# Attention's start, its last weights and its last sums: a reordering on one Trainium2 core

## The chip, the cores and the metric

One core of a Trainium2 chip runs the whole program as a single launch. The metric is the device time of that launch in microseconds (us); lower is better. TensorE is called PE here, VectorE DVE, ScalarE ACT, GpSimd POOL, and SyncE SP; SP issues most of the DMAs.

## The reference

The input `x` holds 64 sequences of 32 positions with 512 features, 2048 rows in all, in fp32. Four layers follow, each `x = x + ffn(cond(x))`. The first is a product chosen per sequence and a feed-forward block, the second a low-rank adapted gated block with a mixture. The change lies in the code of the third and fourth. Cut to what matters:

```python
# layer 2: attention over a paged cache of 512 keys and 32 own keys
q, k = rope(rmsnorm(x @ Wq.T)), rope(rmsnorm(x @ Wk.T))    # 32 and 8 heads of 128
v = x @ Wv.T
s = q @ concat(k_cache[block_table], k).T * SCALE          # masked by length
o = softmax(s) @ concat(v_cache[block_table], v)
y = o @ Wo.T
x = x + (y @ W_base.T + b_base + low_rank_experts(y))      # layer 2's feed-forward
z = einsum('bct,bcd->bdt', x, weights[subjects])           # layer 3
x = x + (z @ W.T + bias + sum_e coeff_e * z @ A_e.T @ B_e.T)
```

## The kernel before, in words

Rows are held in 16 tiles of 128 (`NT`), four sequences to a tile. Layers 0 and 1 come first and end at 1073 us of the profile. Attention follows, and then the tail (`Tail`), which is layer 2's feed-forward and layer 3.

**Attention** works in two halves of the heads, so that there are 32 steps (half, tile), taken in 16 pairs. Projections and output products of a pair are made by a scheme of seven block products (`ORDER`) in place of eight, with sums of blocks ahead of them and of results behind them. Weights and their sums come from HBM in pieces of 512 KB (`wp_piece`, `wo_piece`).

*One turn* is one group of four query heads of one sequence: scores (`scores`, two matmuls, L993), softmax (minimum and mask on DVE L998, exponential on ACT L1000, reciprocal L1002 and scaling L1005 on DVE), four transpositions of the probabilities (`turned`, L707) and the product with the values (`values`, L712). A step has 16 turns, and each turn has two *slots*, into which pieces of other work are put by hand: products of the next pair's projections, output products of the last pair, loads. So a pair has 64 slots. The order on TensorE is written out: `on_pe` chains each matmul to the one before it. On the other engines the Tile framework places instructions by readiness and program order. DMAs that go through `load_by` (L100) are chained on SP, each to be issued behind the last; those that go through `load` or a plain `nc.sync.dma_start` are not.

Keys of a sequence come as 16 pages of 64 KB (`load_keys`), into one of two buffers `kt`; they are asked for when the buffer's last scores have been issued, in slot 2 of each eight and the two behind it (`keys_of`, `later`). Values come by four gathers on POOL (`load_values`, L738).

**The start of attention** (L1093 to L1156) is written out separately, since nothing can hide it: the first pair's 21 products (`products`, seven each of keys and values, first and second query group), the rotations that follow some of them (`rotated`: DVE L782, L770, L785, L771; POOL L786, L130, L787), the transpositions of the rotated keys and queries (`p.turned(g, i, n)`, L707, copied out by ACT), the first pages (`load_keys`), the first values (`values_of`), the copies of the own values (`own_values_of`, eight on DVE, L745), and the first two scores (`start`). Each of `products` makes, per product, two matmuls of 128x512 (four records), an addition or a copy out of PSUM (DVE L872, or ACT L864; PSUM has two such buffers), and asks for the next weight piece.

**The end of attention**: during the last pair there is no next pair to project, and the tail's weights are loaded in five groups (`Tail.weights`, L1303): A3 and B3; W3T; cat2 and B2; base2T; the two biases. In slots 43 to 61 A3 and B3 are multiplied and added to W3T (`scaled`, `fold`). After the last turn `first_sums(nc.vector)` (L925) makes two block sums of the last outputs, ten output products follow, and then the tail runs.

Of the kernel before, what the change touches and what calls it, by code (L numbers as in the profile page):

```python
# [33 lines left out]
P = 128  # L34
# [630 lines left out]
def attention(c, known, x_in, y_part, y_out, sums, tail):  # L665
# [18 lines left out]
    with ExitStack() as outer:  # L684
# [230 lines left out]
        class Outputs:  # L915
# [9 lines left out]
            def first_sums(self, engine):  # L925
                self.o = [oTs.pop(2 * self.n + i) for i in range(2)]
                (_, _), (o21, o22) = self.blocks = [(o[:, :KH, :], o[:, KH:, :]) for o in self.o]
                self.s = qp.tile([P, KH, P], F32, name="o_sum", bufs=1)
                engine.tensor_tensor(self.s, o21, o22, ALU.add)  # L929
                engine.tensor_tensor(o21, self.blocks[0][0], o21, ALU.subtract)  # L930

            def next_sum(self, m, u):
# [182 lines left out]
        def products(n):  # L1115

            for i in range(count[0], count[0] + n):
                p.product(i // 7, p.ORDER[i % 7])
                if i >= 7 and p.ORDER[i % 7] in (7, 4):
                    held.extend(soon)  # L1120
                    del soon[:]
                the_rest()
                if i < 3 * 7 - 8 or i >= 3 * 7 - 4:
                    next_wp()
            count[0] += n
# [1 line left out]
        count = [0]  # L1127
        products(4)
        load_keys(0, 0, range(2))
        products(3)  # L1130
        load_keys(0, 0, range(2, 4))
        with tc.issue_after(p.last_pool):
            values_of(0)
        for i in (0, HKP):
            own_values_of(i)
        products(3)
        p.turned(0, 0, 0)
        products(4)
        new_keys(0, 1)
        load_keys(0, 1, range(2))  # L1140
        p.turned(0, 1, 0)
        p.turned(1, 0, 0)
        own_keys(0, 0, p.kT[0])
        products(1)
        start(0)
        products(1)
        p.turned(1, 0, 1)
        load_keys(0, 1, range(2, 4))
        products(1)
        start(1)  # L1150
        with tc.issue_after(p.last_pool):
            values_of(HKP)
        projections[1].load()
        products(4)
        p.turned(2, 0, 0)

        def slot(fs):
# [9 lines left out]
        for s, (h, T) in enumerate(steps):  # L1167
# [11 lines left out]
            if s % 2 == 0:  # L1179
                if s == 0:  # L1180
                    p = projections[0]
                    at(1, partial(p.turned, 2, 0, 1), partial(own_keys, 0, 1, p.kT[0]))
                    for i, f in zip((2, 4, 6, 8), held):
                        at(i, f)
                    for i, what in ((9, (1, 1, 1)), (11, (1, 1, 0)), (19, (2, 1, 1)), (25, (2, 1, 0))):
                        at(i, partial(p.turned, *what))
                if not last_pair:
                    p = projections[n + 1]
                    if n == 0:
                        ats = ((12, 14, 16, 17, 18, 20, 22), (24, 26, 28, 32, 33, 34, 38),  # L1190
                               (40, 42, 44, 48, 49, 52, 56))
                        then = ((0, 0, 0, 21), (0, 1, 0, 29))
                        for i, f in zip((3, 5, 6, 7, 10), (partial(p.x, 0), partial(p.x, 1), p.x_sums,
                                                           partial(p.tables, "k"), partial(p.tables, "q"))):
                            at(i, f)
                    else:
                        ats = ((2, 4, 10, 12, 14, 18, 20), (22, 28, 30, 34, 36, 38, 40),
                               (42, 44, 46, 50, 52, 54, 58))
                        then = ((0, 0, 0, 13), (0, 1, 0, 27))
                        at(3, partial(p.tables, "q"))  # L1200
                    for *what, i in (*then, (1, 0, 0, 37), (1, 0, 1, 43), (1, 1, 1, 51), (1, 1, 0, 53),
                                     (2, 0, 0, 57), (2, 0, 1, 65), (2, 1, 1, 67), (2, 1, 0, 73)):
                        at(i, partial(p.turned, *what))
                    for g in range(GB):
                        for m, i in zip(p.ORDER, ats[g]):
                            at(i, partial(p.product, g, m), partial(later.append, next_wp))
                            if g and m != 1 and m != 5 and m != 6:
                                at(i, partial(put_off, s * 2 * per + i + 1 + WAIT[m], waiting))
                    if n + 2 < len(projections):
                        then = projections[n + 2]  # L1210
                        for i, f in zip((30, 40, 59, 61, 62), (then.load, partial(then.tables, "k"),
                                                               partial(then.x, 0), partial(then.x, 1),
                                                               then.x_sums)):
                            at(i, f)
                else:
                    for i, f in zip((4, 8, 12, 16, 20), tail.weights(xp, wk, op, wp_tile)):
                        at(i, f)
                    at(43, tail.scaled)
                    for m, i in enumerate((45, 48, 49, 61)):
                        at(i, partial(tail.fold, ps, m))  # L1220
                    at(52, outputs[n].first_blocks)
                    for i, where in enumerate((52, 54, 57, 59)):
                        at(where, partial(outputs[n].product, i), partial(later.append, next_wo))
                if n:
                    out = outputs[n - 1]
                    at(0, partial(out.first_sums, nc.gpsimd))
                    if out.h:
                        at(14, out.befores)
                    ats = (0, 1, 5, 9, 13, 16, 17, 21, 25, 29, 32, 33, 37, 41) if last_pair else \
                        (0, 1, 6, 8, 16, 17, 24, 26, 32, 33, 48, 49, 56, 60)  # L1230
                    for i, where in enumerate(ats):
                        at(where, partial(out.product, i), partial(later.append, next_wo))
                        if i in (5, 7):
                            for u in range(2):
                                at(where, partial(out.next_sum, 6 if i == 5 else 3, u))
                    at(47 if last_pair else 63, out.store)
                else:
                    for i in (40, 46, 52, 58):
                        at(i, next_wo)
# [35 lines left out]
class Tail:  # L1275
# [28 lines left out]
    def weights(self, x_pool, work_pool, pool, pair):  # L1304

        c, nc, a = self.c, self.c.nc, self.c.a

        def updates():
            self.A3 = x_pool.tile([P, 2, KC, P], F32, name="A3", tag="xT").rearrange("p n k f -> p n (k f)")
            self.B3 = x_pool.tile([P, 4, KC // 2, P], F32, name="B3", tag="x_sums") \  # L1310
                .rearrange("p (n a) k f -> p n (a k f)", n=2)
            for t, n in ((self.A3, "A3"), (self.B3, "B3")):
                nc.sync.dma_start(t, a[n].rearrange("(k p) n -> p k n", p=P))

        def square(name):
            src = a[name].rearrange("(k p) n -> p k n", p=P)
            ts = [pair(name) for _ in range(2)]
            for i, t in enumerate(ts):
                nc.sync.dma_start(t, src[:, 2 * i:2 * i + 2, :])
            return [t[:, k, :] for t in ts for k in range(2)]  # L1320

        def last():
            self.w3 = square("W3T")

        def low_rank():
            src = a["cat2"].rearrange("(k p) n -> p k n", p=P)
            n = src.shape[2]
            self.cat = []
            for k in range(0, KC, 2):
                t = work_pool.tile([P, REP, HD], F32, name="cat2", tag="swapped", bufs=2)  # L1330
                t = t.rearrange("p h d -> p (h d)")[:, :2 * n].rearrange("p (k n) -> p k n", n=n)
                nc.sync.dma_start(t, src[:, k:k + 2, :])
                self.cat += [t[:, 0, :], t[:, 1, :]]
            self.wB = work_pool.tile([P, REP, HD], F32, name="B2", tag="squares").rearrange("p h d -> p (h d)")
            nc.sync.dma_start(self.wB, a["B2"])

        def base():
            self.base = square("base2T")

        def biases():  # L1340
            self.bias = {n: c.load(x_pool, n, [P, D], a[n].to_broadcast([P, D]), tag="xt", bufs=2)
                         for n in ("bias2", "bias3")}

        return updates, last, low_rank, base, biases

# [259 lines left out]
```

## Time and profile before

| what | us |
|---|---|
| median of three runs | 3589.3 (3585.83 to 3597.19) |
| profiled execution, its own time | 3603.64 |
| its span | 3601.9 |
| PE busy in it | 3526.7 |
| DVE, POOL, ACT busy in it | 2154.5, 1598.8, 1301.2 |
| idle time of PE that the timeline shows before its instructions | 71.5 |
| of that, from 1073 to 1150 us | about 12 |
| of that, from 3280 to 3440 us | about 16 |
| mean granted TensorE clock | 0.993 |

How to read it: in a timeline a line gives the start, the duration, the engine, the line of the kernel, the operation, the tile written and the tiles read, and the number of merged instructions; a bracket gives the idle time of that engine before it and what ended it. A table by stage gives, per stretch, its length, the busy time and count of PE, of its weight loads, of DVE, ACT and POOL, then the clock that TensorE was granted (1.00 is full), the share of the DMA engines that was busy, and GB/s.

### The profile page before, as it was taken

The page shows a single profiled execution, that of the slowest core. Times are in us where ns is not written, and L with a number is a line of the kernel's source. Part 1 is how long each engine was busy: PE and PEld are TensorE (multiplying, and loading weights), DVE is VectorE, ACT ScalarE, POOL GpSimd, SP SyncE. Part 2 cuts the span into 40 slices and gives each one's busy share as a digit, 9 for nine tenths or more (in the row PEclk, how much of TensorE's full clock was granted, in tenths as well). Part 3 has the DMA queues.
Part 4 walks back from the last instruction along what each step waited for, and adds up shares of the span by engine and source line. Part 5 has one row for each costly group of instructions (what it writes and reads, how often), then busy time and mean ns, then how long its engine had stood idle before and what let it go on. Part 6 is the DMA issues. An engine that isn't in the chain of part 4 may idle for free.

```text
span 3601.9 us, 61460 instructions
## 1 busy us (share of the span) xinstructions
PE 3526.7 (98%) x19328; PEld 2634.1 (73%) x19328; DVE 2154.5 (60%) x5268; ACT 1301.2 (36%) x3110; POOL 1598.8 (44%) x1607
## 2 busy tenths in 40 slices
PE   8999999999998999999999999999999999999999
PEld 3444788877875777787787777877877778777755
DVE  5443222222227777778778677787787777877433
ACT  1111111111113545444454454444544544444311
POOL 0112332222207546456455464564564655644232
PEclk9999999999999999999999999999999999999999
DMA  5003543333226777888877878788878788877731
GB/s 210 27 26 136 174 135 125 103 103 105 101 72 213 249 243 249 256 248 257 255 248 253 258 247 255 249 257 258 255 254 263 245 264 253 256 253 223 217 94 63
DMA packets 610340, 715.99 MB, mean 199 GB/s; under 512 B 61826, under 2 KB 469378, under 8 KB 610018
## 3 DMA queue, kind: packets, MB, share of 16 engines
q1 hardware_dynamic: 557538, 539.01, 48.2%
q0 software_dynamic: 50176, 168.86, 13.4%
q10 hardware_dynamic: 2304, 4.20, 0.3%
q8 instruction: 157, 2.57, 0.3%
q14 instruction: 165, 1.35, 0.1%
HBM read 669.88 MB, written 41.94 MB: 198 GB/s over the span
## 4 chain that ended last, share of the span: by engine, by line
PE 84%; DVE 8%; DMA 3%; issue 2%; POOL 1%; ACT 1%; SPq 1%; DVEq 0%; another core or an unknown queue 0%; ACTq 0%; POOLq 0%
PE po L712 12%; PE gate_up L366 11%; PE py L712 11%; PE sc L993 10%; PE pq L712 7%; PE prT_ps L707 5%; PE pkv L712 5%; PE pz L366 5%; PE po L1371 3%; PE ph L126 3%; PE pd L251 3%; PE po L366 2%; PE qkT_ps L707 1%; PE py L206 1%; DVE pr L1005 1%
## 5 line engine op out<-in xcount | busy, mean ns | idle before, releaser
L738 POOL DMA_INDIRECT vt<-in_v_rows,v_rows x512 | 510.9, 998 | 313.3 <-PE po L712 189.8
L1000 ACT ACTIVATE pr<-pr,low 128x544 f32<-128x544 f32 x512 | 383.3, 749 | 688.1 <-DVE low L998 556.3
L993 PE MATMUL sc<-kt,qT 128*128 128x288 f32 (+1 forms) x2048 | 557.2, 395 | 15.5 <-DVE low L998 12.6
L993 PEld LDWEIGHTS sc<-kt,qT 128*128 128x128 f32 x2048 | 386.2, 191 | 232.2 <-issue 129.3
L712 PE MATMUL po<-prT,vt 128*128 128x128 f32 x4096 | 546.9, 277 | 4.8 <-ACT prT L1011 3.1
L712 PEld LDWEIGHTS po<-prT,vt 128*128 128x128 f32 x4096 | 522.3, 192 | 39.6 <-ACT prT L1011 20.7
L998 DVE CUSTOM_DVE_ANT_0 pr<-sc,mask 128x544 f32<-128x544 f32 x512 | 368.4, 719 | 142.9 <-PE sc L993 119.2
L786 POOL TENSOR_TENSOR projected<-projected,swapped 128x512 f32<-128x512 f32 x160 | 208.3, 1302 | 313.5 <-DVE projected L785 284.5
L1005 DVE TENSOR_SCALAR pr<-pr,low 128x512 f32<-128x512 f32 x512 | 318.4, 622 | 12.6
L1011 ACT COPY prT<-prT_ps 128x512 f32<-128x512 f32 x512 | 294.0, 574 | 75.3 <-PE sc L993 30.8
L707 PE MATMUL prT_ps<-ident,pr 128*128 128x128 f32 x2048 | 312.5, 275 | 1.8 <-DVE pr L1005 1.7
L707 PEld LDWEIGHTS prT_ps<-ident,pr 128*128 128x128 f32 x2048 | 238.5, 142 | 10.4 <-issue 2.1
L712 PE MATMUL py<-wo,oT 128*128 128x256 f32 x1024 | 241.8, 379 | 0.0
L712 PE MATMUL pq<-wp,x_sums 128*128 128x512 f32 x512 | 240.2, 593 | 0.0
L1002 DVE RECIPROCAL low<-low 128x1 f32<-128x1 f32 x512 | 82.1, 160 | 229.7 <-ACT pr L1000 195.3
L712 PEld LDWEIGHTS py<-wo,oT 128*128 128x128 f32 x1024 | 186.5, 190 | 21.1
L1003 ACT ACTIVATE own_pr<-pr,low 128x32 f32<-128x32 f32 x512 | 164.8, 322 | 93.6 <-DVE low L1002 68.5
L452 DVE TENSOR_TENSOR sg<-sg,gate_up 128x256 f32<-128x256 f32 (+1 forms) x88 | 37.0, 421 | 269.3 <-ACT sg L451 265.9
L130 POOL TENSOR_TENSOR rs<-rs,minus_half 128x4 f32<-128x4 f32 x160 | 180.6, 1129 | 23.3 <-DVE low L1002 15.7
L712 PE MATMUL py<-wo,o_sum 128*128 128x256 f32 x768 | 182.9, 382 | 2.3 <-DVE o_sum L929 2.3
L712 PE MATMUL pq<-wp,xT 128*128 128x512 f32 x384 | 182.2, 597 | 0.2 <-issue 0.2
L745 DVE COPY own_vt<-v 32x128 f32<-32x128 f32 x512 | 164.1, 320 | 22.8 <-issue 4.0
(242 smaller groups left out, 5856.2 us busy)
## 6 DMA issues: line engine op xcount, KB each, us to landing
kt<-in_kT SPq DMA_DIRECT2D x2048, 64.0 KB
wp<-in_sums SPq DMA_DIRECT2D x192, 512.0 KB
wo<-out_sums SPq DMA_DIRECT2D x128, 512.0 KB
wp<-in_WqT SPq DMA_DIRECT2D x96, 512.0 KB
wo<-in_WoT SPq DMA_DIRECT2D x96, 512.0 KB
wp<-in_WkT SPq DMA_DIRECT2D x32, 512.0 KB
xt<-x SPq DMA_DIRECT2D x48, 256.0 KB
in_sums<-sums POOLq DMA_DIRECT2D x24, 512.0 KB, 5.1
```

Source lines behind the costliest of these rows:

```text
L130: self.nc.gpsimd.tensor_tensor(t, t, self.minus_half[:, :n], ALU.pow)
L366: c.on_pe(nc.tensor.matmul(out, lhsT, rhs, start=start, stop=stop))
L707: c.on_pe(nc.tensor.transpose(pt[:, m, :], piece, c.ident))
L712: c.on_pe(nc.tensor.matmul(out, lhsT, rhs, start=first and i == 0, stop=last and i == len(pairs) - 1))
L738: nc.gpsimd.indirect_dma_start(out=vts[b % 2][:, n, :], out_offset=None, in_=a["v_rows"], in_offset=bass.IndirectOffsetOnAxis(ap=rows[h][: ...
L786: nc.gpsimd.tensor_tensor(src, src, tmp, ALU.add)
L993: c.on_pe(nc.tensor.matmul(sc[:, lo + n * PSIZE:lo + m * PSIZE].rearrange("p (n k) -> p n k", k=PSIZE), q, kt[:, n:m, g, :], start=True, s ...
L998: nc.vector.tensor_tensor_reduce(pr[:, :NK], sc[:, lo:lo + NK], masks[h, b], -SCALE, 3.0e38, ALU.add, ALU.min, low[:, 0:1])
L1000: nc.scalar.activation(pr[:, :NK], pr[:, :NK], AF.Exp, bias=low[:, 0:1], scale=-1.0, accum_out=low[:, 1:2])
L1003: nc.scalar.activation(own_prs[b % 2][:, g * S:(g + 1) * S], pr[:, L:NK], AF.Copy, scale=low[:, 2:3])
L1005: nc.vector.tensor_scalar(pr[:, :L], pr[:, :L], low[:, 2:3], None, ALU.mult)
L1011: last_prT.append(nc.scalar.copy(prT, pt).ins)
```

## The change

There are three parts.

1. At the start of attention all 14 products of keys, values and the first query group are made before the first transposition; before it was ten, the transposition of the first keys, and four more. The second half of the first pages is asked for after product 9 instead of 7. The own-value copies are placed after product 9, and the first gathers of values after product 14. Behind that the order becomes: one product between each transposition, the first scores after product 17 (15 before), the second after product 20 (17 before). The second sequence's pages, second half, are asked for after product 17 instead of 16.
2. The tail's weight loads all go through `load_by`, and their slots are 6, 14, 38, 46 and 54 instead of 4, 8, 12, 16 and 20. The contents, tiles and tags stay.
3. The first of the last two block sums, where DVE makes it, is made in two halves of 512 elements instead of one of 1024. The sums on POOL, of the other 15 pairs, stay whole.

```diff
-                engine.tensor_tensor(self.s, o21, o22, ALU.add)
+                for q in (slice(0, KH),) if engine is nc.gpsimd else (slice(0, QH), slice(QH, KH)):
+                    engine.tensor_tensor(self.s[:, q], o21[:, q], o22[:, q], ALU.add)
                 engine.tensor_tensor(o21, self.blocks[0][0], o21, ALU.subtract)
...
         products(4)
         load_keys(0, 0, range(2))
-        products(3)
+        products(5)
         load_keys(0, 0, range(2, 4))
+        for i in (0, HKP):
+            own_values_of(i)
+        products(5)
         with tc.issue_after(p.last_pool):
             values_of(0)
-        for i in (0, HKP):
-            own_values_of(i)
-        products(3)
+        new_keys(0, 1)
         p.turned(0, 0, 0)
-        products(4)
-        new_keys(0, 1)
         load_keys(0, 1, range(2))
-        p.turned(0, 1, 0)
-        p.turned(1, 0, 0)
         own_keys(0, 0, p.kT[0])
         products(1)
+        p.turned(0, 1, 0)
+        products(1)
+        p.turned(1, 0, 0)
+        products(1)
+        load_keys(0, 1, range(2, 4))
         start(0)
         products(1)
         p.turned(1, 0, 1)
-        load_keys(0, 1, range(2, 4))
-        products(1)
+        products(2)
         start(1)
         with tc.issue_after(p.last_pool):
             values_of(HKP)
         projections[1].load()
-        products(4)
+        products(1)
         p.turned(2, 0, 0)
...
-                    for i, f in zip((4, 8, 12, 16, 20), tail.weights(xp, wk, op, wp_tile)):
+                    for i, f in zip((6, 14, 38, 46, 54), tail.weights(xp, wk, op, wp_tile)):
                         at(i, f)
...
             for t, n in ((self.A3, "A3"), (self.B3, "B3")):
-                nc.sync.dma_start(t, a[n].rearrange("(k p) n -> p k n", p=P))
+                c.load_by(t, a[n].rearrange("(k p) n -> p k n", p=P))
...
             for i, t in enumerate(ts):
-                nc.sync.dma_start(t, src[:, 2 * i:2 * i + 2, :])
+                c.load_by(t, src[:, 2 * i:2 * i + 2, :])
...
-                nc.sync.dma_start(t, src[:, k:k + 2, :])
+                c.load_by(t, src[:, k:k + 2, :])
...
-            nc.sync.dma_start(self.wB, a["B2"])
+            c.load_by(self.wB, a["B2"])
...
-            self.bias = {n: c.load(x_pool, n, [P, D], a[n].to_broadcast([P, D]), tag="xt", bufs=2)
-                         for n in ("bias2", "bias3")}
+            self.bias = {n: x_pool.tile([P, D], F32, name=n, tag="xt", bufs=2) for n in ("bias2", "bias3")}
+            for n, t in self.bias.items():
+                c.load_by(t, a[n].to_broadcast([P, D]))
```

## The prediction

> **What bounds the kernel now.** I read the page first: TensorE is busy 98% of the span and carries 84% of the chain that ended last.
>
> ```profile
> PE 3526.7 (98%) x19328; PEld 2634.1 (73%) x19328; DVE 2154.5 (60%) x5268; ACT 1301.2 (36%) x3110; POOL 1598.8 (44%) x1607
> PE 84%; DVE 8%; DMA 3%; issue 2%; POOL 1%; ACT 1%; SPq 1%; DVEq 0%; another core or an unknown queue 0%; ACTq 0%; POOLq 0%
> ```
>
> No matmul is added or removed, so the change can win only PE's idle time, 71.5 us by the brackets of its timeline, and the slow matmuls that follow it. I then read PE's timeline where the change works. The start:
>
> ```profile
> 1094.90 0.65 PE L707 MATMUL qkT_ps<-ident,projected 128*128 128x128 f32 x4 [2.08 <-POOL projected L787]
> 1102.97 0.66 PE L707 MATMUL qkT_ps<-ident,projected 128*128 128x128 f32 x4 [0.55 <-POOL projected L787]
> 1107.04 0.66 PE L707 MATMUL qkT_ps<-ident,projected 128*128 128x128 f32 x4 [3.41 <-POOL projected L787]
> 1116.66 5.31 PE L712 MATMUL pq<-wp,x_sums 128*128 128x512 f32 x12
> 1127.91 0.66 PE L707 MATMUL qkT_ps<-ident,projected 128*128 128x128 f32 x4 [1.92 <-POOL projected L787]
> ```
>
> Four transpositions wait for POOL, the last step of a rotation. POOL's own timeline says when those come:
>
> ```profile
> 1088.99 0.94 POOL L738 DMA_INDIRECT vt<-in_v_rows,v_rows  x1 [0.30 <-issue]
> 1089.95 1.12 POOL L130 TENSOR_TENSOR rs<-rs,minus_half 128x4 f32<-128x4 f32 x1
> 1101.89 1.03 POOL L787 TENSOR_TENSOR projected<-projected,rs 128x512 f32<-128x512 f32 x1
> 1105.64 1.35 POOL L787 TENSOR_TENSOR projected<-projected,rs 128x512 f32<-128x512 f32 x1
> 1109.28 1.04 POOL L787 TENSOR_TENSOR projected<-projected,rs 128x512 f32<-128x512 f32 x1
> ```
>
> Five gathers stand ahead of the first rotation, whose DVE part was done at 1082.8. From 1075.9 to 1110.3 POOL has almost no gap: it, not TensorE, sets the rotations' times. What a wait costs beyond itself stands in the table by stage:
>
> ```profile
> 1106.00:1107.00 1.00, 0.00 (x0) 0.00 (x0) 0.78 (x2) 0.00 (x0) 1.00 (x2) 1.00 0.98 387
> 1109.00:1110.00 1.00, 1.00 (x2) 0.34 (x1) 0.00 (x0) 0.00 (x0) 0.92 (x2) 0.50 1.04 418
> 1130.00:1131.00 1.00, 1.00 (x6) 0.99 (x5) 0.60 (x2) 0.05 (x1) 0.00 (x0) 0.50 0.00 0
> ```
>
> After the waits of 3.41 and 1.92 us the clock is 0.50 for about 3.4 us (1108.3 to 1111.7, 1128.9 to 1132.1): 1.7 us lost each time. Last, SP and PE in the last pair, and DVE and PE behind the last turn:
>
> ```profile
> 3321.90 1.83 SPq L1332 DMA_DIRECT2D cat<-in_cat  x2
> 3329.84 11.41 SPq L102 DMA_DIRECT2D kt<-in_kT  x16
> ```
>
> ```profile
> 3341.55 0.72 PE L993 MATMUL sc<-kt,qT 128*128 128x288 f32 x2 [1.99 <-DMA kt<-in_kT]
> 3342.98 0.67 PE L993 MATMUL sc<-kt,qT 128*128 128x256 f32 x2 [0.71 <-DMA kt<-in_kT]
> 3412.01 8.86 PE L712 MATMUL py<-wo,o_sum 128*128 128x256 f32 x32 [2.34 <-DVE o_sum L929]
> ```
>
> ```profile
> 3410.54 1.42 DVE L929 TENSOR_TENSOR o_sum<-oT 128x1024 f32<-128x1024 f32 x1
> 3280.94 8.62 DVE L745 COPY own_vt<-v 32x128 f32<-32x128 f32 x5
> ```
>
> Pages that TensorE needs at 3339.4 are asked for from 3329.84, behind the tail's weights. The block sum holds the first output product for 2.34 us. The last line belongs to a rival.
>
> **Part 1, the start.** Prices from PE's rows: a product 1.72 us (three took 5.31 with the pipeline's end), a transposition of four 0.44, a score 0.92. Products are numbered 1 to 21.
>
> Product 10 ended at 1092.8. Products 11 to 14 then follow at once: 4 x 1.72. One wait comes in: product 11 needs the PSUM buffer of product 9, whose DVE addition ran from 1093.23 to 1093.9, so 1.1. That gives 1100.8. The first transposition, whose input is ready at 1094.9, ends at 1101.2; product 15 at 1103.0; the second transposition (ready at 1102.92) at 1103.4; product 16 at 1105.1. The third is ready at 1107.04 as before, if POOL keeps its order. So the waits of 2.08 and 0.55 go, and one of 1.9 us stands where 3.41 stood, with two more products done.
>
> Before, from 1107.04 to 1127.91 (20.87 us) came seven products, four transpositions, three scores, 1.7 of slow clock and 2.16 of waiting. After, five products, the same four and three: 8.6 + 1.76 + 2.76 = 13.1, so 1120.2. There the transposition of the second group's second block waits for product 19 and its rotation: product 19 ended at 1120.1 before and the transposition began 7.8 later. After, product 19 ends at 1114.0 (1107.48 + 3 x 1.72 + 0.92 + 0.44), plus 7.8 is 1121.8. That is late by 1.6, and it is the new bound. Gain to this point: 1127.91 - 1121.8 = 6.1.
>
> *Clock.* [...] The rows differ: 1.92 and 2.34 us of idling (at 1126 and 3410) also brought 0.50, while 2.08 at 1093 did not. So waits of 1.9 and 1.6 are each a toss-up. The sum of 6.1 has the first spell gone; one spell in two remaining gives the second spell's 1.7 back against it: net +0.8 between -1.7 and +1.7.
>
> *What moves with it.* Eight own-value copies (0.22 each, 1.8 on DVE) pass two products; DVE has the 5.2 us of idling before 1112.07 as cover. Four gathers (about 1.3 each with the issue gap, 5.2 on POOL) pass seven products. They waited for nothing before and POOL took them early, even those of the second sequence that stand far later in the code, so I let POOL's order stay; if they fall behind the rotations, the third transposition is ready sooner, worth up to 1.9 + 1.6. Values are first used at about 1122, and a gather takes 6.2 to land, so they must be issued by 1115. Eight page DMAs on SP (9.9 us at 1090.63) pass two weight pieces, which then land sooner. 14 products at 1.72 want 512 KB each, 305 GB/s, against 260 to 300 moved there; but eight pieces are in place at 1075, and by 1101 only six more (3.1 MB), half the pages (0.5), the rows (0.5) and the gathers (2.1) are needed: 6.2 MB in 24 us, 260 GB/s. No wait charged; bounds 0 and 2.
>
> *Who is late next.* DVE: it was busy 13.3 of 16 us from 1130 to 1146 and stopped PE for 2.05 at 1137. From 1107 to 1146 it idled 11.0 us in all, so it can follow, but not for nothing: I take 0.9 back, with bounds 0 and 4. Part 1: 6.1 + 0.8 - 0.9 = 6.0, from 1 to 10.
>
> **Part 2, the tail's weights.** The same bytes and the same DMAs. Removed ahead of the stalled pages: cat2 and B2 (1.83 + 0.41 on SP) and base2T (0.94), while W3T (about 1.0) takes their place. SP is ready some 2.2 us sooner; in addition W3T's 1 MB no longer runs ahead of the pages before, 2.9 us at the 360 GB/s there. The pages come about 4 us sooner, and TensorE's 1.99 + 0.71 = 2.7 go. In the new places DMA was busy 0.74 to 1.0 (3350 to 3380), then below 0.5; cat2 sits behind finished pages, with eight slots (some 17 us) to the next. The chaining adds a wait: the biases stand behind an output piece that waits for its buffer until about 3389. They are needed by POOL at 3405. Everything later on SP was behind that piece already. I take +2.7; bounds -2.7 (the stall comes back later) and +3.6 (small ACT waits at 3337 and 3324 go too).
>
> **Part 3, halves.** The first half of 512 costs 0.69 by the same engine's L936 rows, instead of 1.42: PE starts 0.7 sooner. Both halves cost the 1.38 that the whole did. [...] The wait becomes 1.6, and the slow clock of 1.6 behind it is again a toss-up: 0.7 + 0.8 = 1.5, bounds 0.5 and 2.3.
>
> **Sum.** 6.0 + 2.7 + 1.5 = 10.2 off the profiled 3603.6 gives 3593.4. That execution is 14.3 above the median of the runs, so I take the gain from the median: 3589.3 - 10.2 = **3579.1**. About 0.3%, 10.8 us, is what a measurement of this kernel can tell from no change; the bound is 3578.5, and the forecast sits on it.
>
> **Rivals.**
> A (54%), the forecast: 3573 to 3585 as its own range, half of it (27%) below the bound.
> B (18%), the gathers fall behind the rotations, and the clock stays full: part 1 gives 6.1 + 1.7 + 3.5 - 0.9 = 10.4, in all 14.6 to 16: 3574. For it: nothing needs the gathers before 1122. Against: POOL took even later ones early.
> C (11%), DVE becomes the bound: part 1 gives about 1, the rest 4.2: 3584. For it: 13.3 of 16 us busy. Against: 11 us of idling.
> D (17%), slower: the own-value copies meet POOL's unbroken run. The row at 3280.94 is this: five copies, 1.1 us elsewhere, took 8.62 while POOL made its sums, and PE then stood 5.67 us and ran 6.8 us at half clock. After the change the eight copies can be due at 1097 or later, amid POOL's run to 1110. If DVE is held there until 1110.3, the evacuations of products wait too: ten products, six transpositions and three scores from 1110.3, 22.6 + 1.7 of slow clock, end at 1134.6 against 1127.9, 6.7 late; the 12.8 us that DVE lost exceed its 11.0 of slack and cost some 6 more, with a second slow spell 3.4. Less part 3, and with part 2's gain lost to a moved stall: about 14 late, 3603. It decides from about 8 us in one hold; below 4 the 1.9 us wait absorbs most. Against: gathers beside the copies did not hold them (0.22 us each at 1085 to 1090).
>
> **How the numbers follow.** Faster by over 0.3%: 27 of A and 18 of B, 45%. Within: 27 of A and 11 of C, 38%. Slower: D, 17%. The range 3568 to 3600 leaves out D's upper part and B's lower end.
>
> **What would show it.** Right: the first transposition begins after 14 products at about 1101 without a wait; one wait of 1 to 2 us ahead of the third; the first values at about 1122.5 instead of 1128.4; no wait for `kt` near 3340; o_sum as two rows of 0.7 and a PE wait of about 1.6. Wrong: an own-value copy of several us, POOL's first rotation after 1090, products that wait for `wp`, or a new `kt` wait after 3350.

## The result and the profile after

| what | before | after |
|---|---|---|
| median of ten runs on the same chip, us | 3588.12 | 3576.89 |
| lowest and highest | 3579.77, 3597.34 | 3570.22, 3587.24 |
| profiled execution, its own time | 3603.64 | 3573.87 |
| PE idle by the brackets of its timeline, each counted once | 68.9 | 55.2 |

The ratio is 0.9967, with a 95% interval of 0.9955 to 0.998. The change gains 11.8 us (7 to 16), where 10.2 were forecast; 3576.9 stands where 3579.1 was put. (The 71.5 us of idling above counts some brackets twice.) The two profiled executions lie 29.8 us apart, and most of that is not the change. By PE's timeline, 9.6 of it stand ahead of attention, where no line was changed, and 6.5 between the second pair's first product and the last projection. Only 3.5 stand at the start. The last pair holds 8.5, which is taken up below, and what follows it 1.6. Of the 9.6, 6.8 are half clock: TensorE was granted 0.50 for 27.3 us ahead of attention in the first execution and for 13.7 in the second.

The first lines of the page, after: PE is idle less, and the chain runs over it for more of the span.

```profile
PE 3511.0 (98%) x19328; PEld 2631.8 (74%) x19328; DVE 2151.2 (60%) x5269; ACT 1297.0 (36%) x3110; POOL 1597.3 (45%) x1607
PE 89%; DVE 4%; DMA 3%; issue 2%; SPq 1%; ACT 1%; DVEq 0%; POOL 0%; ACTq 0%; POOLq 0%
```

The start on PE's timeline. The first product was at 1065.4.

```profile
1084.36 5.42 PE L712 MATMUL pq<-wp,x_sums 128*128 128x512 f32 x12 [1.16 <-DVE projected L872]
1091.33 0.60 PE L707 MATMUL qkT_ps<-ident,projected 128*128 128x128 f32 x4
1095.79 3.62 PE L712 MATMUL pq<-wp,xT 128*128 128x512 f32 x4 [3.86 <-DVE projected L872]
1101.40 0.60 PE L707 MATMUL qkT_ps<-ident,projected 128*128 128x128 f32 x4
1116.41 0.66 PE L707 MATMUL qkT_ps<-ident,projected 128*128 128x128 f32 x4 [0.56 <-POOL projected L787]
```

The first three transpositions wait for nothing now. The wait of 1.16 us ahead of product 11 is there, as forecast, and the transposition of the second group's second block, the last row, waits 0.56. But a wait of 3.86 us that the forecast didn't have stands ahead of product 15, and it is for DVE. DVE's timeline says what DVE did instead of that addition:

```profile
1088.89 2.06 DVE L874 TENSOR_TENSOR projected<-projected 128x512 f32<-128x512 f32 x1
1092.40 2.67 DVE L785 TENSOR_TENSOR projected<-projected,q_cos 128x512 f32<-128x512 f32 x1
1095.06 0.68 DVE L872 TENSOR_TENSOR projected<-pq,projected 128x512 f32<-128x512 f32 x1
```

It finished product 12's sum (L874) and ran its rotation (L785) first, and only then read product 13's result out of PSUM (L872), so that product 15 had no buffer. L874 and L785, which take 0.7 us where nothing holds them, took 2.06 and 2.67 here, beside POOL's rotation steps (L786, L130, L787), which ran without a gap from 1089.13 to 1095.9. The table by stage shows the price behind the wait: half clock.

```profile
1094.00:1095.00 1.00, 0.00 (x0) 0.00 (x0) 1.00 (x2) 0.00 (x0) 1.00 (x2) 1.00 0.75 114
1096.00:1097.00 1.00, 1.00 (x2) 0.48 (x3) 1.00 (x2) 0.00 (x0) 0.99 (x1) 0.50 0.94 371
```

POOL kept its order: its first rotation began at 1080.33, again behind five gathers.

In the last pair, SP's page requests and what PE waited for:

```profile
3299.49 12.41 SPq L102 DMA_DIRECT2D kt<-in_kT  x16
```

```profile
3312.20 0.72 PE L994 MATMUL sc<-kt,qT 128*128 128x288 f32 x2 [1.42 <-DMA kt<-in_kT]
3313.72 0.67 PE L994 MATMUL sc<-kt,qT 128*128 128x256 f32 x2 [0.79 <-DMA kt<-in_kT]
3382.56 8.86 PE L712 MATMUL py<-wo,o_sum 128*128 128x256 f32 x32 [1.75 <-DVE o_sum L930]
```

The pages are asked for 11.3 us before they are needed (3310.8), where it was 9.7. The wait for them is 2.21 us instead of 2.70: shorter, not gone. The last sums hold PE for 1.75 instead of 2.34, with two rows of DVE:

```profile
3381.68 1.43 DVE L930 TENSOR_TENSOR o_sum<-oT 128x512 f32<-128x512 f32 x2
3260.23 2.86 DVE L745 COPY own_vt<-v 32x128 f32<-32x128 f32 x5
```

The second row is the surprise. Five own-value copies of the last pair took 8.62 us before and cost PE a wait of 5.67 and a spell of half clock, about 9 us; the forecast's sum assumed this unchanged. Here they take 2.86, and PE never waits that long.

### The profile page after: what moved, and what is told of

Read it like the earlier page. It is cut to its first block, busy times and chain, and to the rows that moved or that the text cites. A ratio compares the mean times of both kernels' runs of the same rounds, so it can differ in the third digit from the quotient of the medians.

```text
span 3572.1 us, 61462 instructions
## 1 busy us (share of the span) xinstructions
PE 3511.0 (98%) x19328; PEld 2631.8 (74%) x19328; DVE 2151.2 (60%) x5269; ACT 1297.0 (36%) x3110; POOL 1597.3 (45%) x1607
## 4 chain that ended last, share of the span: by engine, by line
PE 89%; DVE 4%; DMA 3%; issue 2%; SPq 1%; ACT 1%; DVEq 0%; POOL 0%; ACTq 0%; POOLq 0%
PE po L712 13%; PE sc L994 11%; PE py L712 11%; PE gate_up L366 11%; PE pq L712 8%; PE prT_ps L707 6%; PE pkv L712 5%; PE pz L366 5%; PE po L1374 3%; PE ph L126 3%; PE pd L251 3%; PE po L366 2%; PE qkT_ps L707 2%; PE py L206 1%; DMA wp<-in_sums 1%
## 5 line engine op out<-in xcount | busy, mean ns | idle before, releaser
L786 POOL TENSOR_TENSOR projected<-projected,swapped 128x512 f32<-128x512 f32 x160 | 208.1, 1301 | 307.3 <-DVE projected L785 284.7
L130 POOL TENSOR_TENSOR rs<-rs,minus_half 128x4 f32<-128x4 f32 x160 | 181.0, 1131 | 23.1 <-DVE low L1003 15.5
L787 POOL TENSOR_TENSOR projected<-projected,rs 128x512 f32<-128x512 f32 x160 | 172.2, 1076 | 7.9
```

The source lines that it names most:

```text
L130: self.nc.gpsimd.tensor_tensor(t, t, self.minus_half[:, :n], ALU.pow)
L786: nc.gpsimd.tensor_tensor(src, src, tmp, ALU.add)
L787: nc.gpsimd.tensor_tensor(src, src, rs.unsqueeze(2).to_broadcast([P, REP, HD]), ALU.mult)
```

## Experiments

Theory: the three parts gain by their own steps, about as forecast, and DVE's order is the new bound at the start. First rival: most of the gain is the vanished stall at those five copies. Twelve kernels ran, in three groups, each on a chip of its own with the kernel before beside it. Gains below are one minus the ratio, times 3588. From a profile, "start" is the time from the first product to the second pair's first product, and "last pair" from the last projection product to the first product with A3 and B3.

**One part, or none.** The four of the first group; the kernel before ran at 3594.79 us on that chip.

Each of the last three takes its part of the diff above whole; of each the line that tells it:

```diff
 e1, part 1
-        products(3)
+        products(5)
...
 e2, part 2
-                    for i, f in zip((4, 8, 12, 16, 20), tail.weights(xp, wk, op, wp_tile)):
+                    for i, f in zip((6, 14, 38, 46, 54), tail.weights(xp, wk, op, wp_tile)):
...
 e3, part 3
-                engine.tensor_tensor(self.s, o21, o22, ALU.add)
+                    engine.tensor_tensor(self.s[:, q], o21[:, q], o22[:, q], ALU.add)
```

> The kernel before, unchanged, profiled once more. Theory 1 (the hold of the own-value copies in the last pair, 8.62 us in the first profile and 5.67 us of TensorE idling, is a matter of a microsecond of phase between DVE and POOL): this profile may well lack it, and then the five copies take under 3 us and TensorE idles under 2 us there. Rival 2 (it belongs to the kernel before, and the change removes it): 8.6 and 5.7 us again. Both: time within 0.2% of the kernel before; layers 0 and 1 end some us apart from the 1073.1 us of the first profile.

> Part 1 alone. Theory 1 (part 1 carries the gain, cut by a DVE wait): 4 to 6 us faster than before; from the first product to the first product of the next pair 70.5 us instead of 74.0; a wait of about 3.9 us ahead of product 15 for the DVE addition of product 13. Rival (the forecast's sum): 6 us, and the large wait stands ahead of the third transposition. Rival 2 (the gain lies in the last pair): under 2 us faster.

> Part 2 alone. Theory 1 (the pages are still late, since W3T's 1 MB now stands just ahead of them): 0 to 1 us faster, and TensorE's waits for pages in the last pair stay at 2.0 to 2.4 us instead of 2.7. Rival (the forecast's step): 2.7 us faster and no wait for pages. Rival 2 (part 2 removes the hold of the own-value copies in the last pair): 5 to 10 us faster.

> Part 3 alone. Theory 1: TensorE's wait ahead of the first product of the last sums falls from 2.34 to 1.75 us and the slow clock behind it stays (1.7 us): 0.6 us faster, which the times cannot show. Rival (the forecast's toss-up falls well): the slow clock goes too, 2.3 us faster.

| kernel | us | ratio (95%) | start | wait for pages | last sums, PE's wait | five copies |
|---|---|---|---|---|---|---|
| before again | 3596.45 | 1.0009 (0.9999 to 1.002) | 70.3 | 2.81 + 1.02 | 2.49 | 8.66 |
| part 1 | 3591.48 | 0.9989 (0.998 to 0.9998) | 70.5 | 2.81 + 1.54 | 2.27 | 8.65 |
| part 2 | 3589.02 | 0.9988 (0.9979 to 0.9997) | 74.1 | 1.09 | 3.14 | 8.68 |
| part 3 | 3595.24 | 0.9994 (0.9984 to 1.0005) | 74.0 | 2.97 + 1.44 | 1.61 | 8.73 |

The parts alone gain 3.9 us (0.7 to 7.2), 4.3 (1.1 to 7.5) and 2.2 (-1.8 to 5.7). Part 1 showed the wait of 3.87 us ahead of product 15, as its first expectation had it. Part 2 fits none of its three expectations: the gain is above the forecast's 2.7, yet 1.09 us of waiting for pages stayed. The stall stood in all four profiles at the same place with the same length. So it isn't a chance of the single execution. The kernel before showed two courses of its start, one of 74.0 and one of 70.3 us, with the same program.

**The order at the start, and the place of W3T.** The second group; the kernel before at 3587.48 us.

```diff
 e4, in products, ahead of the rotations
+                if i == 11:
+                    behind.extend(soon)
+                    del soon[:]
+                if i == 14:
+                    soon.extend(behind)
 e5
-zip((6, 14, 38, 46, 54), tail.weights(...))
+zip((6, 30, 38, 46, 54), tail.weights(...))
 e6, twice; turn_end holds the last step of the rotation placed last (L787)
-        with tc.issue_after(p.last_pool):
+        with tc.issue_after(turn_end[0]):
```

> The change, with the rotation that follows product 12 put behind product 15, so that DVE empties PSUM of product 13 first. Theory 1 (DVE's order made the wait of 3.86 us ahead of product 15): that wait falls under 1 us, the slow clock behind it (1.7 us) goes, and the third transposition waits for POOL instead, 1 to 2 us; 3 to 5 us faster than the change, so 14 to 16 below the kernel before. Rival (DVE is short of time whatever its order): the wait moves a few products on, under 1 us gained.

> The change, with W3T loaded in slot 30 instead of 14. Theory 1 (what stood ahead of the late pages is W3T now, 1 MB on busy DMA engines): TensorE's waits for pages near 3312 (1.42 and 0.79 us) and the slow clock behind them (1.7 us) go, 2 to 4 us faster than the change. Rival (the pages are late because their buffer comes free late): the waits stay within 0.5 us of 2.2, no gain.

> The change, with the eight gathers of values tied behind the rotation of product 12 on POOL. Theory 1 (rotations come sooner, and DVE is held less by POOL where it meets it, but the DVE additions bound the start): 1 to 4 us faster than the change. Rival B of the forecast: no wait of over 1 us before the first values, 5 us faster. Rival (the values come late): a wait for values, slower than the change.

> The change once more, beside the three above. Theory 1: its start as in the first profile (wait of 3.9 us ahead of product 15, 70.5 us from the first product to the next pair's first), its page waits 1.5 to 2.5 us, while the own-value copies of the last pair take anything from 2 to 9 us. Rival 2 (the change removes their hold): they take under 3 us again. Time 9 to 13 us below the kernel before.

| kernel | us | ratio (95%) | start | wait for pages | five copies |
|---|---|---|---|---|---|
| the changed kernel again | 3577.81 | 0.9975 (0.9963 to 0.9987) | 71.4 | 1.05 + 1.31 | 2.86 |
| product 12's rotation behind product 15 | 3576.86 | 0.9971 (0.9957 to 0.9984) | 67.4 | 3.35 | 2.86 |
| W3T in slot 30 | 3578.7 | 0.9975 (0.9964 to 0.9986) | 72.2 | 2.13 + 1.96 | 2.87 |
| the gathers behind the rotations | 3568.73 | 0.9954 (0.9938 to 0.997) | 66.3 | 0.25 + 2.53 | 2.86 |

With DVE's order put right, the 3.86 us wait falls to 0.27, and the largest left ahead of the first values is 1.51, at product 16. PE's timeline, rotation behind product 15:

```profile
1090.72 1.98 PE L712 MATMUL pq<-wp,xT 128*128 128x512 f32 x4 [0.27 <-DVE projected L872]
1094.66 1.98 PE L712 MATMUL pq<-wp,xT 128*128 128x512 f32 x4 [1.51 <-DVE projected L872]
```

By time this gains 10.4 us, 1.4 more than the changed kernel beside it; the 3 to 5 more that were expected can't be seen in the noise, and the third transposition did not wait for POOL. The same wait shrinks if, instead, POOL makes the gathers later. PE's timeline of that kernel at products 11 to 13 and at product 15:

```profile
1083.86 5.42 PE L712 MATMUL pq<-wp,x_sums 128*128 128x512 f32 x12 [0.67 <-DVE projected L873]
1092.52 1.98 PE L712 MATMUL pq<-wp,xT 128*128 128x512 f32 x4 [1.09 <-DVE projected L873]
```

This is rival B's order made real. Its working gave 14.6 to 16 us in all; the run gained 16.5 (11 to 22), though the clock did not stay full at the start, as B had it: 3.4 us of half clock followed the first values. The two DVE rows that had stretched ran at their usual length there, with the rotation still ahead of the addition: L785 took 0.68, and L874 of the profile above, one line further down in this kernel, 0.69 instead of 2.06. So most of the 3.86 us came of the stretching; with the order alone, 1.09 was left. Other rows of DVE were longer there (two own-value copies took 0.96 and 1.32).

```profile
1088.39 0.69 DVE L875 TENSOR_TENSOR projected<-projected 128x512 f32<-128x512 f32 x1
```

W3T out of the way of those pages changed little: 2.13 us of waiting for them was left, where the changed kernel beside it had 2.36. So W3T's place isn't what leaves the wait. Behind W3T's new place a second wait of 1.96 stood at later scores (3356.15); the profile puts it down to issue.

**Two parts, and both orders.** The third group; the kernel before at 3586.95 us.

The pairs are the edits of e1, e2 and e3 put together by two. Both orders are the changed kernel with two edits from above:

```diff
+                if i == 11:
+                    behind.extend(soon)
+                    del soon[:]
+                if i == 14:
+                    soon.extend(behind)
...
-        with tc.issue_after(p.last_pool):
+        with tc.issue_after(turn_end[0]):
```

> Parts 1 and 2, with the last block sum whole. In every profile so far with at most one of the parts, five own-value copies in the last pair took 8.6 us and TensorE stood 5.7 us (last projection product to the tail's first folding product: 103 to 110 us); in every one with all three it did not (95 to 98 us). Theory 1: the stall goes with the tail's loads being out of the way together with the other place of the start's loads, so parts 1 and 2 suffice: no copy over 3 us, 95 to 98 us, and 3580, ratio 0.997 to 0.998. Theory 2: it is the layout of the instructions, so each part, also part 3, counts: the stall can stay, 105 us, ratio 0.9975 to 0.999 (sum of the parts alone, 3.9 and 4.3 us). In both TensorE's wait at the last sums is 2.3 us again.

> Parts 1 and 3; the tail's loads as before. Theory 1 (parts 1 and 2 are needed): the copies in the last pair take 8.6 us, TensorE stands 5.7 us, last projection to first fold 106 to 110 us, ratio 0.998 to 0.999. Theory 2 (layout; part 3 counts): the stall can be gone, 98 us, ratio near 0.9965. In both the tail's pages are waited for by 2.8 and 1.4 us as before, and the last sums show two rows of 0.7.

> Parts 2 and 3; the start as before (first product to pair 2's first product 71 to 74 us). Theory 1 (parts 1 and 2 are needed): the stall of 8.6 us stays, last projection to first fold 103 us as with part 2 alone, ratio 0.998 to 0.999. Theory 2 (layout; part 3 counts): the stall can be gone, 95 to 98 us, ratio near 0.9965.

> The changed kernel with both orders at the start put right: the gathers behind product 12's rotation on POOL, and that rotation behind product 15 on DVE. Theory: both took the same wait away (first product to first values 51.5 us in the changed kernel, 48.4 with one, 47.3 with the other, no wait over 1.5 us left in either), so together they give 46 to 47 us, no more than 1 us below the better one: ratio 0.9945 to 0.996, 3568. Rival: DVE and POOL block each other, so that each order alone only moves the wait; together 43 to 45 us, 3564. If the last gather lands late instead, a new wait for the values of 1 to 3 us appears.

| kernel | us | ratio (95%) | start | wait for pages | last sums, PE's wait | five copies |
|---|---|---|---|---|---|---|
| parts 1, 2 | 3583.24 | 0.9988 (0.9977 to 1.0) | 72.2 | 3.04 | 2.52 | 2.85 |
| parts 1, 3 | 3584.98 | 0.9992 (0.9983 to 1.0002) | 71.6 | 5.25 + 2.38 | 1.61 | 2.86 |
| parts 2, 3 | 3580.19 | 0.9983 (0.9973 to 0.9993) | 70.7 | 0.24 + 2.85 | 1.61 | 2.86 |
| both orders | 3571.97 | 0.9955 (0.9941 to 0.9968) | 66.4 | 3.17 | 1.87 | 2.86 |

The theory that parts 1 and 2 are needed to end the stall fell: every pair was without it. The theory that the layout of the instructions does it didn't hold either. It would have let the pairs without part 2 or part 1 gain the stall's 9 us on top of their own, and parts 1 and 3 gained 2.9 us in all, less than the 6.1 that they gained one by one. What the profiles with the stall share is plainer. Four of the five came from one chip, on which the kernel before itself took 3594.79 us, and the nine without it include all eight of the two chips where it took 3587.48 and 3586.95. The 7 to 8 us between the chips is about the stall, and they are not the clock: the runs' spans times their granted clocks average 3572.5 us on the first chip and 3566.0 and 3566.3 on the others, each with a standard error of 0.4. But the profiles also divide by the number of parts: none or one with the stall, two or three without. Only the times speak for the chip. A profile of the kernel before on the other two chips would settle it; none was taken. The chip of the first two profiles isn't known.

How the stall comes about can be seen by setting two kernels side by side whose code differs only in attention's start: part 3 alone, then parts 1 and 3. From 3240 us on, the rows of PE, DVE, ACT and POOL come in the same order and at the same times within 0.03 us in both, up to the rows below. ACT's and DVE's timelines in the first, DVE's in the second:

```profile
3268.74 0.58 ACT L1042 COPY oT<-po 128x512 f32<-128x512 f32 x1 [0.96 <-PE prT_ps L707]
3269.45 0.69 DVE L1042 COPY oT<-po 128x512 f32<-128x512 f32 x1 [0.93 <-PE prT_ps L707]
3270.17 8.73 DVE L745 COPY own_vt<-v 32x128 f32<-32x128 f32 x5
```

```profile
3268.53 0.69 DVE L1042 COPY oT<-po 128x512 f32<-128x512 f32 x1
3269.25 2.86 DVE L745 COPY own_vt<-v 32x128 f32<-32x128 f32 x5
```

In the first, ACT and DVE leave their wait for PE 1 us late. The copies then begin 0.65 us after POOL's step at L130 (3269.52) instead of 0.25 before it (3269.50). POOL's timeline in the first, that step and its two block sums:

```profile
3269.52 1.04 POOL L130 TENSOR_TENSOR rs<-rs,minus_half 128x4 f32<-128x4 f32 x1
3274.06 2.34 POOL L930 TENSOR_TENSOR o_sum<-oT 128x1024 f32<-128x1024 f32 x1
3276.48 2.34 POOL L931 TENSOR_TENSOR oT<-oT 128x1024 f32<-128x1024 f32 x1
```

Three of the five copies are held: the first until the step behind L130 ends (3271.8), the fourth for 4.13 us until the first block sum ends (3276.4), the fifth until the second ends (3278.8). The other two took 0.22 each, beside a gather. The same meeting stands in all five profiles with the stall: DVE waits 0.93 to 1.05 us and the copies begin 0.65 to 0.77 us after L130. In the nine without it they begin 0.24 or 0.25 before it. The fourth copy was held through the last step of POOL's rotation (L787, 1.05 us at 3273.06) and the block sum behind it (2.34), not through one instruction. What the two engines meet at, no trace here shows; the rows show only that the three copies end with POOL's instructions. Why the wait ended late stays open.

With both orders the start is 66.4 us, no better than the gathers' order alone (66.3), which fits the theory that the two edits take away the same wait. The expectation of 46 to 47 us to the first values was missed by 0.4 (47.4), and the rival that each order only moves the wait fell. The fastest kernel is the changed one with its gathers behind the rotations, 3568.73 us, 0.9954 of before; both orders together, at 0.9955, can't be told from it.

## Why the prediction was right, and where its steps were not

The sum was right. The ratios of the parts, the pairs and the two runs of the whole, fitted by least squares as three numbers that add, give 2.5, 4.3 and 2.1 us, each with a standard error of 1.1. They sum to 8.8 and leave no deviation beyond the runs' own spread. So the parts add up, and no stall that comes or goes with the change is needed to explain the times. The first rival fell as a cause of the measured gain; in the difference of the two profiles it is the largest item within the changed code. That the sum came so near is in part luck: part 1 fell short by 3.5, and the other two came out higher by 2.2, which their standard errors alone could make.

**Part 1: 6.0 forecast, 2.5 found.** The order of the steps was right as far as product 14: the wait of 1.1 came as 1.16, product 14 ended 25.96 us after the first began (25.8 forecast), POOL kept its order, no own-value copy of the start took over 0.4 us, and rival D did not occur. What failed is "product 15 at 1103.0". It took PE from one transposition to the next product with no other condition than PE's own, and left out that product 15 needs the buffer of product 13, as product 11 needs that of product 9. The late addition behind DVE's 2.06 and 2.67 us cost 3.86 and about 1.7 of half clock; the first values came 51.5 us after the first product, where 47.5 were forecast and 53.4 stood before. "Who is late next" had the right engine and the right kind of cost, and priced it at 0.9 with bounds 0 and 4: rival C's mechanism, DVE as the bound, is what happened, by DVE's order and its meetings with POOL more than by its load. The two runs with that wait undone show it: the start falls from 71.4 to 67.4 and 66.3. The wait of 1.9 at the third transposition did not come, and that of 1.6 at the second group's second block came as 0.56, since PE arrived late itself. Two of the six profiles with the changed start took another course, with waits of about 2.76, 0.97 and 2.67 us for DVE ahead of products.

The base was mis-sized too. Without part 1 the start took 74.0 or 74.1 us in three profiles and 70.3 and 70.7 in two, and the forecast was worked out on one of 74.0. Over the profiles the start takes 72.6 us on average without part 1 (five) and 71.4 with it (six, the ones with an edited order left out).

**Part 2: 2.7 forecast, 4.3 found.** The direction was right and the picture was not. "TensorE's 1.99 + 0.71 = 2.7 go" failed: with part 2 the wait was 1.09 to 4.09 us in nine profiles. But without part 2 it was larger than the first profile's 2.70 in every other one, 3.83 to 4.41 us with the stall and 7.63 without it. The stall itself delays PE, so that with it SP had asked for the pages 8.7 to 9.9 us ahead of PE's need, and without it only 7.3. That profile, parts 1 and 3, shows what the old places of the weights cost:

```profile
3312.16 14.19 SPq L102 DMA_DIRECT2D kt<-in_kT  x16
```

```profile
3324.67 1.30 PE L994 MATMUL sc<-kt,qT 128*128 128x288 f32 x2 [5.25 <-DMA kt<-in_kT]
3328.35 1.19 PE L994 MATMUL sc<-kt,qT 128*128 128x256 f32 x2 [2.38 <-issue]
```

The last pair took 103.3 us there and 95.4 to 100.2 with part 2 and no stall; with the stall, 102.9 with part 2 and 105.8 to 109.6 without. The wait after 3350 that the forecast's lower bound allowed for did not come in the changed kernel.

**Part 3: 1.5 forecast, 2.1 found.** The halves took 0.7 each where nothing disturbed them. PE's wait was 2.27 to 3.14 us in the five profiles without part 3 and 1.61 to 2.28 in the nine with it. The spell of half clock behind it stayed in three of the nine (32 matmul records in 8.8 us) and fell away in six (7.2): a toss-up, as forecast. Part 3's own gain is not clear of noise.

Taking the gain from the median and not from the profiled time was right: 3593.4, the profile's own time less the sum, would have missed by 16.5 us.

## What to carry to other kernels

When products or steps are moved together, write down for each one not only its inputs but the PSUM buffer that it needs, and which instruction on which engine frees it; here the framework ran a rotation ahead of the addition that frees the buffer, and PE waited 3.86 us. Before costing an edit on one profile, ask whether the same program shows the same course twice: here the unchanged start differed by 3.7 us, as much as a part of the change, and a stall by 9. And try parts alone and in pairs by time, not by one profile each, since a profile's difference may belong to the chip it was taken on (the kernel before took 7 to 8 us more on one), or to where half clock fell in that one execution (27.3 us of it ahead of attention in one, 13.7 in another).

## What the hardware showed that was not expected

A wait of 1.75 us ahead of the last sums brought half clock, while one of 2.28, and one of 2.52, did not. What decided in these traces is where the wait lies. In each of the fourteen traces all spells of half clock begin on one grid of 3.41 us, whose place differs from execution to execution. Of the grid's windows at full clock, all 77 in which PE idled 2.0 us or more were followed by a window at 0.50, and none with less than 1.69 us was; in between, 26 were and 15 were not. Here the wait of 1.75 us lies in one window (the table by stage of the change, first), and that of 2.28 is cut by the grid (the same table with the gathers behind the rotations, second):

```profile
3379.19:3382.60 3.41, 1.67 (x22) 1.35 (x21) 1.61 (x3) 0.58 (x1) 2.48 (x2) 1.00 0.05 19
3382.60:3386.02 3.42, 3.42 (x8) 2.77 (x9) 1.73 (x2) 0.00 (x0) 0.00 (x0) 0.50 0.00 0
```

```profile
3371.66:3375.07 3.41, 2.25 (x24) 1.94 (x24) 0.81 (x2) 0.87 (x3) 1.79 (x2) 1.00 0.25 92
3375.07:3378.49 3.42, 2.12 (x10) 1.89 (x11) 3.16 (x4) 0.00 (x0) 0.69 (x1) 1.00 0.00 0
```

The window behind the last row was at full clock too. So in these traces a wait of about 2 us was a toss-up because its place on the grid was.

Beside rotation steps on POOL, DVE's 0.7 us instructions took up to 2.67 us, and one unlucky meeting stretched five copies from 2.86 to 8.7. The sixteen page requests took SP 9.3 us to issue at 3314 in the changed kernel and 14.2 at 3312 in the one with parts 1 and 3, 0.58 and 0.89 each.
